# Counting subsets of both node halves with one pair of matmuls in a one-core graph network kernel

## The chip, the cores and the metric

The kernel runs on one core of a Trainium2 chip. The metric is the device time of one execution in microseconds (us). Three runs of the kernel before took 6450.48, 6465.61 and 6453.73 us, so its median is 6453.73 us. The engines are named as the profile names them: PE is the matrix engine (PEld its weight loads), DVE the vector engine, ACT the scalar engine, POOL the general engine that here also issues one DMA queue, and SP the engine that issues most other DMAs. PSUM is the memory that PE writes; it has eight banks of 512 fp32 columns on 128 partitions.

## The reference

There are 16 graphs of 1024 nodes with 128 features and a dense 0/1 adjacency matrix each. Four layers follow one another, each as `x = layernorm(x + layer(x, adj))`. Layer 0 is masked attention, layer 2 a sum over neighbours with a two-layer network, layer 3 a three-step convolution on a thinned adjacency matrix. The change touches layer 1 only:

```python
p = jnp.einsum('bnd,do->bno', x, W1 - W2)
q = jnp.einsum('bnd,do->bno', x, W2)
pre = p[:, :, None, :] + q[:, None, :, :] + b
h = jax.nn.relu(pre) * adj[..., None]
return jnp.max(h, axis=2)
```

For each node and feature this is the maximum of `q` over the node's neighbours, added to `p`, with a floor of zero. A maximum over a masked set of 1024 rows is not a matrix product, and the kernel finds it in another way.

## The kernel before, in words

The neighbours are taken in groups of six. A group has 64 subsets. For each group the kernel keeps a table with the maximum of `q` over each of the 64 subsets (128 features by 64 subsets), and for each node it needs the one entry that stands for the node's own neighbours in that group. Two groups (12 neighbours) make a slot: one on partitions 0 to 63, the other on partitions 64 to 127. A graph has `NP` = 86 slots, and all graphs together 16 x 86 = 1376.

One slot has these steps; the line numbers are those of the profile.

- `count` (L792): a matmul of a constant table of plus and minus ones, `lit`, with 120 rows of the transposed adjacency matrix, `AT`, gives for each subset and node the count of agreeing neighbours in `pm` (L799). ACT turns it into a one-hot row, `relu(count + 1 - size)`, written to `hot` (L800); the constant is the bias operand `one_less`. This is done twice in a slot, for nodes 0 to 511 and for nodes 512 to 1023, which are called its two halves, h = 0 and h = 1.
- `table` (L802), once in two slots: two PE transposes bring two slots' tables from `sub` into the PSUM tile `pt` (L811), and ACT copies it, rounded, to `high` (L814).
- `low_part` (L817): a matmul with minus the identity subtracts `high` from `pt` where it stands (L819), and ACT copies the rest to `low` (L821). `pt` so stays in its bank from `table` until `low_part` of the next slot's first half.
- `look_up` (L824), once for each half: four matmuls (L830) multiply `hot` by `high` and by `low`. The two groups lie on partitions 0 to 63 and 64 to 127 and use the two row halves of PE's array, into two banks of `pg`. DVE then keeps the running maximum in `best` (L890), 128x1024 in one instruction.

PSUM is laid out by tags: `wide` has two buffers of two banks for `pg`, `shared` two banks for the other layers, and `subset` two banks that `pm` and `pt` take in turn.

The counting runs two slots ahead of the look-up. The order of all work of PE, ACT, DVE and POOL in this stage is written out by the function `slot`: in each half come the look-up, then pieces of the other layers' work for PE ("streams": attention of the next graph, layer 2 of the last graph, and the thinning of the adjacency matrix, "dilation"), then their pieces for ACT and DVE, then `low_part`, `count` and `table`, then the maximum. Each engine runs its list strictly in that order, and an engine that waits for another holds up all that stands behind.

Chunks of `AT`, 120 rows for 10 slots, are loaded by POOL's DMA queue (L751), which converts fp32 to fp8. There are nine chunks for a graph (the last has 64 rows, and POOL clears its tile first, L750), four buffers, and a load is issued two chunks ahead of its use. The same engine, POOL, computes the row-by-row thinning (L658 to L668) and issues the loads of `An` and `E`.

After the 1376 slots come layer 3's passes over all graphs, which the change does not touch.

Of the kernel before, what the change touches and what calls it, by code (L numbers as in the profile page):

```python
# [29 lines left out]
F32 = mybir.dt.float32  # L30
F32R = mybir.dt.float32r
BF = mybir.dt.bfloat16
F8 = mybir.dt.float8e4
F16 = mybir.dt.float16
AF = mybir.ActivationFunctionType
# [4 lines left out]
B, N, D, H2 = 16, 1024, 128, 256  # L40
P = 128
T = N // P
GS = 6
PS = 2 * GS
PC = 10
CH = PC * PS
NP = -(-N // PS)
TG = 12
R, G = 32, 4
# [11 lines left out]
def subset_tables():  # L61

    half = P // 2
    s = np.arange(half)
    lit = np.zeros((CH, PC, P), np.float32)
    for j in range(CH):
        a, k = divmod(j % PS, GS)
        lit[j, j // PS, a * half:(a + 1) * half] = np.where((s >> k) & 1, 1.0, -1.0)
    size = sum((s >> k) & 1 for k in range(GS))
    return lit, np.tile(1.0 - size, 2).astype(np.float32).reshape(P, 1)  # L70


@with_exitstack
def tile_graph_layers(ctx: ExitStack, tc, a, out):
    nc = tc.nc
    x, adj, adjT = a["x"], a["adj"], a["adjT"]
    halves = (slice(0, 512), slice(512, 1024))

    consts = ctx.enter_context(tc.tile_pool(name="consts", bufs=1))
    dram = ctx.enter_context(tc.tile_pool(name="dram", bufs=1, space=DRAM))  # L80
    small = ctx.enter_context(tc.tile_pool(name="small", bufs=3))
    psum = None
# [9 lines left out]
    psum = setup.enter_context(tc.tile_pool(name="psum0", bufs=2, space=PSUM))  # L92
# [9 lines left out]
    nc.vector.memset(ones_b, 1.0)  # L102
    mhalf = consts.tile([P, T], F32, name="mhalf")
    nc.vector.memset(mhalf, -0.5)
    lit = consts.tile([CH, PC, P], F8, name="lit")
    nc.gpsimd.dma_start(out=lit, in_=a["lit"])
    less = consts.tile([P, P], F32R, name="less")
    nc.vector.tensor_scalar_mul(less, ident, -1.0)
    one_less = consts.tile([P, 1], F32, name="one_less")
    nc.sync.dma_start(out=one_less, in_=a["one_less"])  # L110

    def weight(name, shape=(P, P), how=None, pool=consts):
        t = pool.tile(list(shape), F32, name="w_" + name)
# [49 lines left out]
    pm = bank("pm")  # L163
# [5 lines left out]
    for b in range(B):  # L169
        q, g = divmod(b, G)  # L170
        nc.gpsimd.dma_start(out=half_rows[g * R:(g + 1) * R, :, q],
                            in_=a["nodemask"][b].rearrange("(k r) -> r k", r=R))
# [65 lines left out]
    def layers_012():  # L238
# [3 lines left out]
        psum = psums.enter_context(tc.tile_pool(name="psumA", bufs=1, space=PSUM))  # L242
        apool = es.enter_context(tc.tile_pool(name="apool", bufs=1))
# [500 lines left out]
        def load_columns(at):  # L744
            b, c = divmod(at, T + 1)
            if b < B:
                rows = min(CH, N - c * CH)
                t = AT[at] = apool.tile([CH, N], F8, name="AT", bufs=4)
                if rows < CH:
                    nc.gpsimd.memset(t, 0.0)  # L750
                nc.gpsimd.dma_start(out=t[:rows], in_=adjT[b, c * CH:c * CH + rows])  # L751

        An, AT, subs, qs, ps, values, exps, bests, hots, tables = ({} for _ in range(10))
        now, taken, given, held = 0, 0, {}, {}
        pending = {}
# [33 lines left out]
                        given[held[stream]] = now + 0.5  # L789
                    pending[stream] = [next(stream, None), now]  # L790

        def count(s, h):  # L792

            b, g = divmod(s, NP)
            c, r = divmod(g, PC)
            if h == 0:
                hots[s] = w2.tile([P, N], F32R, name="hot", bufs=3)
            pm = psum.tile([P, 512], F32, tag="subset", name="pm", bufs=2)
            nc.tensor.matmul(pm, lit[:, r, :], AT[b * (T + 1) + c][:, halves[h]], start=True, stop=True)  # L799
            nc.scalar.activation(hots[s][:, halves[h]], pm, AF.Relu, bias=one_less)  # L800

        def table(s):  # L802

            b, g = divmod(s, NP)
            g0 = g - g % TG
            assert ("sub", b, g0) in happened, (s, [(x.__name__, pending[x]) for x in streams], room)
            pt = psum.tile([P, 512], F32, tag="subset", name="pt", bufs=2)[:, :2 * P]
            if g + 2 - g0 == min(TG, NP - g0):
                happened["used", b, g0] = now
            for k in range(2):  # L810
                nc.tensor.matmul(pt[:, k * P:(k + 1) * P], subs[b, g0][:, g - g0 + k, :], ident, is_transpose=True,  # L811
                                 start=(k == 0), stop=(k == 1))
            high = w2.tile([P, 2 * P], F32R, name="high", bufs=2)
            nc.scalar.copy(high, pt)  # L814
            tables[s] = pt, high

        def low_part(s):  # L817
            pt, high = tables[s]
            nc.tensor.matmul(pt, less, high, start=False, stop=True, skip_group_check=True)  # L819
            low = w2.tile([P, 2 * P], F32R, name="low", bufs=2)  # L820
            nc.scalar.copy(low, pt)  # L821
            tables[s] = high, low

        def look_up(s, h, pg):  # L824

# [23 lines left out]
        def slot(s, last):  # L849

            nonlocal now
            now = s
            b, g = divmod(s, NP)
            if s >= 0 and g == 0:
                finish(b)
                if b + 1 < B:
                    start(tables_of(b + 1), True)
                    load_x(b + 1)
                    start(attend(b + 1))
                    start(scores(b + 1))  # L860
                if b:
                    start(rest(b - 1))
            if s >= 0 and g % PC == 0:
                load_columns(b * (T + 1) + g // PC + 2)
            for h in range(2):
                now = s + 0.5 * h
                for e in ROOM:
                    room[e] = min(room[e] + ROOM[e] / 2, ROOM[e])
                if s >= 0:
                    pg = psum.tile([P, 2, 512], F32, tag="wide", name="pg", bufs=2)  # L870
                    look_up(s, h, pg)
                early = s >= 0 and due < now
                if early:
                    dilate_on()
                advance(("PE",))
                advance(("A", "V", "Pool"))
                if s >= 0 and not early:
                    dilate_on()
                if h == 0 and s % 2 and s + 1 < last:
                    low_part(s + 1)  # L880
                if s + 2 < last:
                    count(s + 2, h)
                    if h and s % 2 == 0:
                        table(s + 2)
                if s >= 0:
                    own = bests[b][:, :, halves[h]]
                    if g == 0:
                        nc.vector.tensor_copy(own, pg)
                    else:
                        nc.vector.tensor_max(own, own, pg)  # L890
            if s >= 0:
                hots.pop(s)
# [1 line left out]
        dilate = dilation()  # L894
        due, wants_bank = 0.0, False
        load_x(0)
        for at in range(2):
            load_columns(at)
        front, back = scores(0), attend(0)
        for t in range(T):  # L900
            while ("e", 0, t) not in happened:
# [6 lines left out]
        first = tables_of(0)  # L908
# [2 lines left out]
        start(first, True)  # L911
        with tc.manual_schedule(engines={mybir.EngineType.PE, mybir.EngineType.Activation, mybir.EngineType.DVE,
                                         mybir.EngineType.Pool}):
            for s in range(-2, B * NP):
                slot(s, B * NP)
            finish(B)
        assert not streams, streams
# [316 lines left out]
```

## Time and profile before

| What | Value |
| --- | --- |
| profiled execution, its own time | 6458.95 us |
| its span, first to last instruction | 6457.2 us |
| median of the three runs | 6453.73 us |
| the slots' stage, first transposition of a table to the last one-hot | 129.9 to 5163.4 us, 5033.5 us |
| one slot, mean | 5033.5 / 1376 = 3.66 us |
| granted PE clock, whole span and slots' stage | 0.934 and 0.94 |
| first counting matmul | 36.8 us |

The profile is one execution. Busy time is given as the union of an engine's instructions, so a group with two matmuls at a time counts once. A PE matmul's recorded duration includes the time until its results are written, which overlaps the next matmul; so the distance from one start to the next says what a matmul costs PE, and a PE that is 92% busy in this sense still has room. "Idle before, releaser" says what ended an engine's idle time.

### The profile page before, as it was taken

Reading aid. Unit: us, or ns where it says so; the run is one execution under the profiler, and the core shown is the slowest. Engines: PE = TensorE matmul, PEld = TensorE weight load, DVE = VectorE, ACT = ScalarE, POOL = GpSimd, SP = SyncE. Lnnn points to the kernel's source line nnn. Section 1 sums busy time; section 2 is a strip of 40 time slices with the busy share of each in tenths; the row PEclk is TensorE's granted clock in tenths of the full one; section 3 lists DMA queues with packets and bytes.
Section 4 is the critical chain, followed back from the end, with each engine's and each line's share of the span. In section 5 each row is a group of like instructions: output and inputs, shape, how many; then the busy total and the mean of one; then the engine's idle time right before and its main releaser. Section 6 shows DMA issues by size and latency. Waiting matters only on the chain. (4 is left out here: it accounts for less than half of the span.)

```text
span 6457.2 us, 90620 instructions
## 1 busy us (share of the span) xinstructions
PE 5729.3 (89%) x29184; PEld 2962.2 (46%) x29354; DVE 4978.8 (77%) x7877; ACT 3946.3 (61%) x7142; POOL 3502.1 (54%) x11319
## 2 busy tenths in 40 slices
PE   6989999989899999999989998989998867877998
PEld 3444444444444444444444444444443335555654
DVE  3888888888888888888888888888888834444445
ACT  4667666666667666766666666666665623333755
POOL 2665766666666666766666666666666511110113
PEclk8989899999899999999999999998998988888999
DMA  5121212121212121212121212121211065654545
GB/s 38 13 30 21 35 21 36 21 34 21 34 21 37 20 35 20 34 20 32 24 34 20 34 20 34 20 35 20 35 21 18 20 101 106 126 103 111 206 167 186
DMA packets 478402, 317.32 MB, mean 49 GB/s; under 512 B 301162, under 2 KB 429668, under 8 KB 473828
## 3 DMA queue, kind: packets, MB, share of 16 engines
q0 software_dynamic: 105648, 84.20, 15.0%
q1 hardware_dynamic: 367600, 226.13, 11.9%
q8 instruction: 230, 3.77, 0.2%
q10 hardware_dynamic: 4676, 1.19, 0.1%
q14 instruction: 248, 2.03, 0.1%
HBM read 412.71 MB, written 117.18 MB: 82 GB/s over the span
## 5 line engine op out<-in xcount | busy, mean ns | idle before, releaser
L890 DVE TENSOR_TENSOR best<-best,pg 128x1024 f32<-128x1024 f32 x2720 | 3258.7, 1215 | 556.8 <-PE pg L830 546.8
L800 ACT ACTIVATE hot<-pm,one_less 128x512 fp32r<-128x512 f32 x2752 | 1882.7, 689 | 736.9 <-PE pm L799 727.5
L830 PE MATMUL pg<-hot,high 64*128 64x512 f32 x5504 | 1436.1, 519 | 239.2 <-DVE best L890 231.4
L830 PE MATMUL pg<-hot,low 64*128 64x512 f32 x5504 | 1139.8, 411 | 0.0
L799 PE MATMUL pm<-AT,lit 120*128 120x512 fp8e4 x2752 | 1110.3, 404 | 20.9 <-ACT hot L800 8.5
L830 PEld LDWEIGHTS pg<-hot,high 64*128 64x128 f32 x5504 | 533.6, 191 | 1018.9 <-DVE best L890 510.5
L830 PEld LDWEIGHTS pg<-hot,low 64*128 64x128 f32 x5504 | 553.0, 198 | 0.0
L658 POOL TENSOR_SCALAR sc<-low_counts,half_mask,rest 16x1 f32<-16x1 f32 x992 | 351.8, 355 | 323.7 <-DVE rest L644 218.8
L799 PEld LDWEIGHTS <-lit 120*128 120x128 fp8e4 x2752 | 272.6, 99 | 520.5 <-issue 460.2
L663 POOL TENSOR_SCALAR sc<-sc 16x1 f32<-16x1 f32 x992 | 397.3, 401 | 105.1
L821 ACT CAST low<-pt 128x256 fp32r<-128x256 f32 x688 | 256.1, 372 | 258.2 <-PE pt L819 255.0
L1039 POOL TENSOR_TENSOR length<-length,mhalf 128x8 f32<-128x8 f32 x48 | 78.9, 1644 | 570.8 <-DVE length L1038 570.8
L660 POOL TENSOR_SCALAR sc<-sc 16x1 f32<-16x1 f32 x992 | 315.0, 318 | 107.7
L819 PE MATMUL pt<-high,less 128*128 128x256 f32 x688 | 294.1, 427 | 85.0 <-ACT high L814 78.2
L703 POOL TENSOR_SCALAR shifts<-centre 128x4 f32<-128x4 f32 x32 | 10.5, 327 | 656.9 <-DVE width L699 633.6
L665 POOL TENSOR_SCALAR hit<-V,sc 16x31 bf16<-16x31 bf16 (+30 forms) x992 | 361.1, 364 | 0.0
L666 POOL TENSOR_SCALAR last_rank<-V,sc 16x31 f32<-16x31 bf16 (+30 forms) x992 | 344.5, 347 | 0.0
L996 ACT CAST m<-near 128x1024 fp32r<-128x1024 fp8e4 x256 | 253.4, 1044 | 112.6 <-DVE near L965 59.6
L475 DVE TENSOR_TENSOR sub<-sub,q 128x24 f32<-128x24 f32 (+11 forms) x768 | 303.3, 396 | 24.0 <-ACT q L297 10.4
L811 PE MATMUL pt<-ident,sub 128*128 128x128 f32 x1376 | 286.1, 291 | 26.7 <-ACT hot L800 22.3
L385 PE MATMUL pav<-v,eT 128*128 128x128 f32 x2048 | 301.7, 293 | 2.1 <-ACT eT L378 2.1
L1009 PE MATMUL pagg<-m,high 128*128 128x512 f32 x768 | 277.3, 432 | 13.2 <-ACT high L1002 13.2
(268 smaller groups left out, 9754.6 us busy)
## 6 DMA issues: line engine op xcount, KB each, us to landing
removed<-gone SPq DMA_DIRECT2D x128, 256.0 KB
An<-in_adj_dram POOLq DMA_DIRECT2D x16, 1024.0 KB, 14.8
E<-in_adj_dram POOLq DMA_DIRECT2D x128, 128.0 KB, 5.8
gone_all<-removed POOLq DMA_DIRECT2D x64, 256.0 KB, 12.3
near<-in_adjT_dram POOLq DMA_DIRECT2D x16, 1024.0 KB, 17.9
kept<-near SPq DMA_DIRECT2D x16, 1024.0 KB
share<-share SPq DMA_DIRECT2D x32, 512.0 KB
hidden<-r SPq DMA_DIRECT2D x32, 512.0 KB
```

The costliest lines, as they stand in the source:

```text
L385: nc.tensor.matmul(pav, eT[:, c, :], values[b][:, c, :], start=(c == 0), stop=(c == T - 1))
L475: nc.vector.tensor_max(sub[:, :n_g, n:2 * n], sub[:, :n_g, 0:n], qg[:, 2 * g0:2 * g0 + n_g, k:k + 1].to_broadcast([P, n_g, n]))
L658: gp.tensor_scalar(half, mine, half_mask[:, m], rest[:, n:n + 1], op0=ALU.mult, op1=ALU.add)
L660: gp.tensor_scalar(sf, half, 5.5, sf, op0=ALU.is_gt, op1=ALU.mult)
L663: gp.tensor_scalar(to, at, sf, none, op0=ALU.subtract, op1=ALU.subtract)
L665: gp.tensor_scalar(hit[:, n, n + 1:], V[:, n, n + 1:], at, None, op0=ALU.is_equal)
L666: gp.tensor_scalar(last[:, n + 1:], V[:, n, n + 1:], to, None, op0=ALU.is_le)
L799: nc.tensor.matmul(pm, lit[:, r, :], AT[b * (T + 1) + c][:, halves[h]], start=True, stop=True)
L800: nc.scalar.activation(hots[s][:, halves[h]], pm, AF.Relu, bias=one_less)
L819: nc.tensor.matmul(pt, less, high, start=False, stop=True, skip_group_check=True)
L830: nc.tensor.matmul(pg[:, a], part[rows, at * P:(at + 1) * P], hots[s][rows, halves[h]], start=(k == 0), stop=(k == 1))
L890: nc.vector.tensor_max(own, own, pg)
```

## The change

`count` is done once for a slot. `lit` and `AT` become bf16 and are laid out anew: 60 neighbour rows of nodes 0 to 511 lie on partitions 0 to 59, and the same 60 neighbour rows of nodes 512 to 1023 on partitions 64 to 123. `lit` has the same table on both. Partitions 60 and 124 of `AT` hold ones, and those of `lit` the constant `1 - size`, so the bias operand goes. The two matmuls of 61 rows stand one after the other and are given the two row halves of PE's array; they write the two banks of one two-bank tile `pm`, and one ACT instruction of 128x1024 makes the whole `hot`.

That tile is the only buffer of the tag `subset`. The table can no longer stay in its bank between `high` and `low`, so the tables are transposed twice: once for `high` (`high_part`), and once more, one slot later, for `low` (`low_part`), followed at once by the subtraction. In a slot `count` stands at the end of the first half, and `high_part` (odd slots) or `low_part` (even slots) at the end of the second. `high_part` stands one slot earlier than `table` did, and the stage's loop begins one slot earlier.

The chunks of `AT` have two buffers in place of four, whose rows of ones are set once, and are loaded one chunk ahead in place of two. A chunk is two DMAs (four for a graph's last chunk), and the clearing of the last chunk's tile is gone. Two one-row DMAs of `one_less` into `lit` come at the start.

```diff
-    lit = consts.tile([CH, PC, P], F8, name="lit")
+    lit = consts.tile([P, PC // 2, P], BF, name="lit")
     nc.gpsimd.dma_start(out=lit, in_=a["lit"])
+    for part in range(2):
+        nc.gpsimd.dma_start(out=lit[64 * part + SUB:64 * part + SUB + 1],
+                            in_=a["one_less"].rearrange("(o r) m -> o r m", o=1))
...
-                t = AT[at] = apool.tile([CH, N], F8, name="AT", bufs=4)
-                if rows < CH:
-                    nc.gpsimd.memset(t, 0.0)
-                nc.gpsimd.dma_start(out=t[:rows], in_=adjT[b, c * CH:c * CH + rows])
+                t = AT[at] = columns_in[at % len(columns_in)]
+                for part, s in enumerate(halves):
+                    whole = rows // SUB
+                    first = c * CH + whole * SUB
+                    nc.gpsimd.dma_start(out=t[64 * part:64 * part + SUB, :whole],
+                                        in_=adjT[b, c * CH:first, s].rearrange("(j r) m -> r j m", r=SUB))
...
+        columns_in = [apool.tile([P, 2, 512], BF, name=f"AT{i}") for i in range(2)]
+        for t in columns_in:
+            nc.vector.memset(t, 1.0)
...
-            pm = psum.tile([P, 512], F32, tag="subset", name="pm", bufs=2)
-            nc.tensor.matmul(pm, lit[:, r, :], AT[b * (T + 1) + c][:, halves[h]], start=True, stop=True)
-            nc.scalar.activation(hots[s][:, halves[h]], pm, AF.Relu, bias=one_less)
+            pm = both_banks("pm")
+            for part in range(2):
+                rows = slice(64 * part, 64 * part + SUB + 1)
+                nc.tensor.matmul(pm[:, part], lit[rows, r, :], AT[b * (T + 1) + c][rows, j, :], start=True, stop=True)
+            nc.scalar.activation(hots[s], pm.rearrange("p h n -> p (h n)"), AF.Relu)
...
+        def both_banks(name):
+            return psum.tile([P, 2, 512], F32, tag="subset", name=name, bufs=1)
...
+        def high_part(s):
+            pt = turned(s)
+            tables[s] = w2.tile([P, 2 * P], F32R, name="high", bufs=2)
+            nc.scalar.copy(tables[s], pt)
...
         def low_part(s):
-            pt, high = tables[s]
-            nc.tensor.matmul(pt, less, high, start=False, stop=True, skip_group_check=True)
+            pt = turned(s)
+            nc.tensor.matmul(pt, less, tables[s], start=False, stop=True, skip_group_check=True)
...
-                load_columns(b * (T + 1) + g // PC + 2)
+                load_columns(b * (T + 1) + g // PC + 1)
...
-                if h == 0 and s % 2 and s + 1 < last:
-                    low_part(s + 1)
-                if s + 2 < last:
-                    count(s + 2, h)
-                    if h and s % 2 == 0:
-                        table(s + 2)
+                if h == 0:
+                    if 0 <= s + 2 < last:
+                        count(s + 2)
+                elif s % 2:
+                    if s + 3 < last:
+                        high_part(s + 3)
+                elif s + 2 < last:
+                    low_part(s + 2)
```

`turned` is the part of the old `table` that takes the PSUM tile and does the two transposes (L811).

## The prediction

> **What bounds the kernel now.** I read the page first, then the slots' stage by itself, then the waits, and last PE's own list in order of time.
>
> ```profile
> L890 DVE TENSOR_TENSOR best<-best,pg 128x1024 f32<-128x1024 f32 x2720 | 3258.7, 1215 | 556.8 <-PE pg L830 546.8
> L800 ACT ACTIVATE hot<-pm,one_less 128x512 fp32r<-128x512 f32 x2752 | 1882.7, 689 | 736.9 <-PE pm L799 727.5
> ...
> L819 PE MATMUL pt<-high,less 128*128 128x256 f32 x688 | 294.1, 427 | 85.0 <-ACT high L814 78.2
> ...
> L811 PE MATMUL pt<-ident,sub 128*128 128x128 f32 x1376 | 286.1, 291 | 26.7 <-ACT hot L800 22.3
> ```
>
> ```profile
> core 0: us, PE busy (x) PEld busy (x) DVE busy (x) ACT busy (x) POOL busy (x), PEclk, DMA share, GB/s
> 130.00:5163.00 5033.00, 4597.58 (x24012) 2257.17 (x24178) 4362.48 (x6692) 3333.43 (x6298) 3266.30 (x10896) 0.94 0.19 26
> ```
>
> In the slots' stage (the second view) PE is recorded busy 91% of the time, DVE 87%, ACT 66%, POOL 65%. A slot takes 3.66 us; DVE has 4362.5 / 1376 = 3.17 us of work in it. In this view neither PE nor DVE alone is full: they wait for each other in turn, since `pg` has only two buffers.
>
> ```profile
> POOL shifts L703 <- DVE width L699: 633.6, 31, 33.2
> ...
> DVE best L890 <- PE pg L830: 546.8, 951, 7.7
> PEld pg L830 <- DVE best L890: 510.5, 920, 5.8
> ...
> PE pg L830 <- DVE best L890: 231.4, 238, 5.5
> ```
>
> The waits give total, times and the longest, in us. DVE waited for PE 951 times and a weight load of PE for DVE 920 times. So a microsecond saved or added on PE reaches the end only where PE is the later of the two, roughly every second time. ACT is off the path save where PE waits for a bank (78.2 and 22.3 us).
>
> ```profile
> 2505.49 0.38 PE L799 MATMUL pm<-AT,lit 120*128 120x512 fp8e4 x1
> 2505.80 0.50 PE L830 MATMUL pg<-hot,high 64*128 64x512 f32 x2
> 2506.14 0.40 PE L830 MATMUL pg<-hot,low 64*128 64x512 f32 x2
> 2506.47 0.39 PE L799 MATMUL pm<-AT,lit 120*128 120x512 fp8e4 x1
> 2506.79 0.50 PE L830 MATMUL pg<-hot,high 64*128 64x512 f32 x2
> 2507.12 0.40 PE L830 MATMUL pg<-hot,low 64*128 64x512 f32 x2
> 2507.45 0.82 PE L427 MATMUL pa<-An,parts 128*128 128x512 fp8e4 x3
> 2508.11 0.38 PE L799 MATMUL pm<-AT,lit 120*128 120x512 fp8e4 x1
> 2508.33 0.38 PE L811 MATMUL pt<-ident,sub 128*128 128x128 f32 x2
> 2508.64 0.50 PE L830 MATMUL pg<-hot,high 64*128 64x512 f32 x2
> ```
>
> The lines give start and duration in us. From start to start: a count before a look-up costs PE 0.32 us (2506.47 to 2506.79), before another full-array matmul 0.22; a look-up pair 0.33; two transposes 0.31. A half with nothing between count and count but a look-up lasts 0.98 us (2505.49 to 2506.47).
>
> **The change, part by part.** "Gross" is what PE gains or loses; "passed" what reaches the end.
>
> 1. PE's work. In two slots four counts become two pairs. A pair costs what one count did, if it runs as the look-up's pairs do (x2 in 0.33 us). Two counts go, 2 x 0.32, and one pair of transposes comes, 0.31: 0.33 us less for two slots, 688 x 0.33 = 227 us gross. Setting each of DVE's waits before L890 against what PE would save ahead of it, the smaller of the two sums to 88 us (0.083 us in each half) or 168 us (0.165). I take -130.
>
> 2. Row halves next to row halves. The count before a look-up costs 0.10 us more than before a full-array matmul, and the step from look-up to count 0.33, 0.11 more than 0.22. In some 20% of slots no stream work lies between look-up and count in the first half, and there both extras go: 1376 x 0.20 x 0.21 = 58 us gross, between 0 and 58; taken -30. The Trainium skill (TensorEngine Tiling (Array Packing), Tiling Modes, Key Properties) says that a change of tiling mode drains the array; by that rule the whole 58 us goes. The rows show the 0.10 and 0.11 us, but not what a bf16 pair costs beside the fp32 one.
>
> 3. The old wait of the subtraction for `high` (78.2 us) goes, since `high` is copied a slot earlier. By the same half, -45 (between 0 and -78).
>
> 4. The new wait. With one buffer, `turned` at the end of the second half cannot start until ACT has read all of `pm`, which PE wrote half a slot earlier. The new ACT instruction is not in the trace. ACT's relu from PSUM without bias takes 597 ns for 512 columns (L323), and 1114 ns against 687 ns is the step from 512 to 1024 columns with a bias (L1025, L299): 597 + 427 = 1.02 us. From the pair's start it is 0.39 (matmul) + 0.04 (ACT starts 37 ns after PE's end) + 1.02 + 0.055 (PE starts after ACT) = 1.50 us before PE may transpose. PE gets there after 0.98 us where only a look-up lies between. Lined up slot by slot in the trace, the time from a slot's first count to its second had quartiles 0.99, 1.59 and 1.98 us. With each first one-hot's end put 0.33 us later (1.02 for 0.69), PE would come too early in 59% of slots, and wait 424 us gross. Behind the waiting transposes stand the next slot's look-up on PE, and DVE's maximum behind that. Where DVE was still busy at that maximum the wait is covered: taking its slack off leaves 225 us passed at once. Below: ACT has 0.36 us a slot less to do (2 x 0.689 - 1.02), so a one-hot that stood behind other ACT work starts sooner; 0.2 us sooner leaves 282 gross, 140 passed. Above: all 424. I take +225, as lateness not passed at once is in part passed later.
>
> 5. A second wait: the next count must wait until ACT has copied `high` or `low` out of the same tile, and that copy (0.37 us) stands behind the second half's stream work on ACT. Lined up likewise: 57 us gross in 8% of slots, 27 passed; taken +27.
>
> 6. ACT's saving, 0.36 x 1376 = 495 us busy, is worth nothing by itself: ACT already waits 727.5 us for counts.
>
> 7. Loads. 144 issues at 0.66 us become 16 x (8 x 2 + 4) = 320: 116 us more on POOL, less 16 clearings of 0.94. That is 3.3 us in each of 31 blocks of thinning, under the 20 us that POOL waits for `width` in each (633.6 / 31): 0. A chunk is asked for 8 slots (29 us) ahead, a graph's first chunk 4 slots (14.6 us), and needs two issues and a landing, 2 x 0.66 + 3.8 = 5.1 us. POOL issued the four-slot loads between 18 us before and 4 us after their slot began: covered. (Near the end it was up to 22 us late, against 29 us.) If that cover went, each load late by 1 us would stop PE's count and cost up to 143 us in all. POOL ahead of its slot now waits for PE's last count in the buffer that it refills, and the thinning rows behind it lose only lead. SP loses one issue.
>
> 8. The start. Two one-row issues and a wait for `lit` to land stand ahead of POOL's other loads; ACT waited 5.6 us for the first `An`. Between 0 and 8 us, taken +3. DVE's two memsets and the extra first slot fall into this idle time.
>
> Sum: -130 - 30 - 45 + 225 + 27 + 3 = +50 us on the profiled 6458.95, 6509; the median of the runs lies 5.2 us lower, so 6505 us, 0.8% slower.
>
> Against this change the Trainium skill speaks twice (Perfetto Trace Analysis): Optimizing Tensor Performance, Matmuls, wants independent matmul groups to rotate through PSUM banks so that evacuation overlaps the next group, and Optimizing Scalar/DVE Operations wants larger instructions where the engine is saturated and smaller ones where an unsaturated engine makes others wait. ACT at 66% is the latter; by the rule the bubble stays whole, 424 + 57 in place of 225 + 27, and the time would be 6733. The trace has DVE cover half of it.
>
> **Rivals.**
>
> - Faster: the wait mostly does not come. For it: ACT's list gets shorter, and it waited 727.5 us for counts. Against it: 0.98 against 1.50 us in the shortest halves, which no shorter ACT queue mends. It decides where the wait passes less than the 205 - 30 = 175 us of items 1 to 3 less items 5 and 8. At 140 passed, nothing for item 5 and all of 168, 58 and 78: -161, 6293; halfway to the forecast about 6400.
> - Much slower: PE becomes later than DVE nearly everywhere, and all of items 4 and 5 passes: 424 + 57 - 130 - 30 - 45 + 3 = +279, 6733. For it: one tile makes PE and ACT alternate in every half. Against it: DVE's 3.17 us of work a slot.
> - The pairs do not overlap, so a pair costs 0.22 more: 1376 x 0.22 = 303 gross, half passed, about 6655. Against it: the look-up's pairs on the same row halves.
> - Loads late: 143 loads by 1 to 3 us, 6600 to 6900. Against it: item 7.
>
> **How the numbers follow.** This kernel's measurement can tell 0.3%, 19 us, from no change. Chances: forecast 0.48 (0.39 of it slower, 0.08 same, 0.01 faster), faster rival 0.27 (0.26 faster, 0.01 same), much slower 0.18, pairs 0.03, loads 0.04. Together slower 0.64, same 0.09, faster 0.27. The range, 6370 to 6690, leaves out a tenth on each side: the faster rival's far half and the upper part of the slower ones. The forecast's own range is 6440 to 6610.
>
> **What would show it.** In the changed profile: the relu of 128x1024 near 1.02 us; counts x2 with 0.33 us to the look-up; a wait "PE pt <- ACT hot" of 300 to 450 us in place of 22.3, mostly behind halves without streams; no wait of the subtraction for `high`; DVE's wait for `pg` above 546.8 us; ACT near 55% in the stage; no wait of a count for a DMA. The prediction is wrong if the wait for `hot` stays under 150 us, if a look-up after a count starts later than 0.4 us, or if a count waits for a load.

## The result, and the profile after

The changed kernel took 6508.34 us (median of 4 runs, 6502.60 to 6518.97) against 6454.54 us (4 runs, 6450.48 to 6465.61) for the kernel before: a ratio of 1.0083, 95% interval 1.0064 to 1.0101, so 54 us or 0.8% slower. The prediction was 6505. The profiled execution was the longest of the four, 6518.97 us, with a span of 6515.7 us. The times below are those of fast executions; one of the four of e10_apart_noturn took 9151.69 us and is left out of its time.

The page of the changed kernel, its first line and the costliest groups of instructions (busy time, mean ns of one, then the idle time before them and its releaser):

```profile
span 6515.7 us, 92909 instructions
...
L912 DVE TENSOR_TENSOR best<-best,pg 128x1024 f32<-128x1024 f32 x2720 | 3264.2, 1215 | 620.3 <-PE pg L850 604.8
L815 ACT ACTIVATE hot<-pm 128x1024 fp32r<-128x1024 f32 x1376 | 1407.1, 1023 | 815.4 <-PE pm L814 811.9
...
L824 PE MATMUL pt<-ident,sub 128*128 128x128 f32 x2752 | 611.8, 306 | 465.9 <-ACT hot L815 460.7
...
L814 PE MATMUL pm<-AT,lit 61*128 61x512 bf16 x2752 | 570.6, 410 | 30.2 <-ACT high L831 22.6
```

The single ACT instruction for a slot's one-hots takes 1023 ns, and PE's transpositions now wait 460.7 us for it, where the same row of the kernel before had 22.3. No row of the subtraction (L835) waits for `high` any more, and no count waits for a load.

Busy times in the slots' stage of the changed kernel:

```profile
core 0: us, PE busy (x) PEld busy (x) DVE busy (x) ACT busy (x) POOL busy (x), PEclk, DMA share, GB/s
130.00:5220.00 5090.00, 4327.59 (x25537) 2309.62 (x25537) 4365.11 (x6679) 3001.71 (x4920) 3385.42 (x11055) 0.93 0.19 29
```

PE's busy share fell from 91% to 85% and ACT's from 66% to 59%, and yet the stage is longer. DVE's work is what it was, 4365 against 4362 us.

The waits of the changed kernel (total, times, longest, in us):

```profile
PEld pt L824 <- ACT hot L815: 898.9, 1041, 2.8
ACT hot L815 <- PE pm L814: 811.9, 808, 4.2
DVE best L912 <- PE pg L850: 604.8, 1008, 9.7
...
POOL shifts L705 <- DVE width L701: 532.9, 32, 27.5
PE pt L824 <- ACT hot L815: 460.7, 713, 2.3
...
PEld pg L850 <- DVE best L912: 309.5, 377, 5.8
...
PE pg L850 <- DVE best L912: 209.1, 210, 5.6
...
POOL AT L754 <- PE pm L814: 126.9, 29, 21.4
```

DVE waits longer for PE than before (604.8 against 546.8), and PE's weight loads wait less for DVE (309.5 against 510.5): PE is now the later of the two more often, by a wait that was 22.3 us before.

PE's list in order of time (start, duration, in us):

```profile
2500.93 0.39 PE L814 MATMUL pm<-AT,lit 61*128 61x512 bf16 x2
2500.97 0.59 PE L850 MATMUL pg<-hot,high 64*128 64x512 f32 x2
2501.39 0.39 PE L850 MATMUL pg<-hot,low 64*128 64x512 f32 x2
2502.52 0.44 PE L824 MATMUL pt<-ident,sub 128*128 128x128 f32 x2 [0.74 <-ACT hot L815]
2502.89 0.50 PE L850 MATMUL pg<-hot,high 64*128 64x512 f32 x2
```

Two things are to be seen. A pair of counts costs PE very little in front of a look-up: from its start to the `low` pair 0.46 us, where one count had 0.65 (2505.49 to 2506.14 in the kernel before). And the transposition starts 1.59 us after the counts, though PE could have been there after 0.46 + 0.33 = 0.79.

**Where the time went, on PE's own row.** The steps from the start of one PE matmul to the start of the next add up to the whole time. I read these steps from the records between 400 and 4800 us. A step's own length was taken as the shortest usual one between the same two neighbours (the 5th percentile over all kernels of this study; for the step to a `low` pair behind a count the median, 0.42, since it scatters); the rest of a step is lateness of the matmul that ends it. In us per slot, with some of the experiments told below:

```
                              before  after  e1_apart  e2_first  e8_later  e9_both  e7_full
time of a slot                 3.706  3.730     3.568     3.756     3.670    3.623    3.702
PE's own work                  3.073  2.741     2.715     2.820     2.653    2.610    3.181
late: transpositions           0.049  0.446     0.173     0.200     0.181    0.098    0.088
late: subtraction              0.083  0         0         0         0        0        0
late: look-up (high pair)      0.241  0.267     0.369     0.305     0.329    0.372    0.204
late: counts                   0.061  0.047     0.091     0.160     0.272    0.273    0.052
the rest                       0.199  0.229     0.220     0.271     0.235    0.270    0.177
```

The change took 0.332 us a slot of work off PE (457 us over 1376 slots) and 0.083 of the old wait (114 us), and it added 0.397 us of lateness of the transpositions (546 us). These nearly cancel; the look-up, the counts and the rest make the small difference. The rows of lateness hardly depend on how the neighbours are grouped, but the line between PE's own work and the rest does: grouped otherwise, up to 0.1 us a slot moves from one to the other, and the work saved comes to 0.29 to 0.34. The stage lost its time gradually, and none in its last third: set against the kernel before, slot 86 ended 12 us later, slot 600 32 us, slot 946 58 us, slot 1375 59 us, and layer 3 behind it took as long as before.

### The profile page after: what moved, and what is told of

The parts are those of the page before. It is cut to its first block, busy times and chain, and to the rows that moved or that the text cites. A ratio compares the mean times of both kernels' runs of the same rounds, so it can differ in the third digit from the quotient of the medians.

```text
span 6515.7 us, 92909 instructions
## 1 busy us (share of the span) xinstructions
PE 5461.6 (84%) x30730; PEld 3014.8 (46%) x30730; DVE 4987.6 (77%) x7879; ACT 3616.6 (56%) x5766; POOL 3623.7 (56%) x11481
## 5 line engine op out<-in xcount | busy, mean ns | idle before, releaser
L912 DVE TENSOR_TENSOR best<-best,pg 128x1024 f32<-128x1024 f32 x2720 | 3264.2, 1215 | 620.3 <-PE pg L850 604.8
L815 ACT ACTIVATE hot<-pm 128x1024 fp32r<-128x1024 f32 x1376 | 1407.1, 1023 | 815.4 <-PE pm L814 811.9
L850 PE MATMUL pg<-hot,high 64*128 64x512 f32 x5504 | 1566.9, 565 | 217.0 <-DVE best L912 209.1
L850 PE MATMUL pg<-hot,low 64*128 64x512 f32 x5504 | 1153.8, 415 | 0.0
L824 PE MATMUL pt<-ident,sub 128*128 128x128 f32 x2752 | 611.8, 306 | 465.9 <-ACT hot L815 460.7
L850 PEld LDWEIGHTS pg<-hot,high 64*128 64x128 f32 x5504 | 558.8, 199 | 502.8 <-DVE best L912 309.5
L824 PEld LDWEIGHTS pt<-ident,sub 128*128 128x128 f32 x2752 | 312.7, 147 | 947.6 <-ACT hot L815 898.9
L814 PE MATMUL pm<-AT,lit 61*128 61x512 bf16 x2752 | 570.6, 410 | 30.2 <-ACT high L831 22.6
L831 ACT CAST high<-pt 128x256 fp32r<-128x256 f32 x688 | 255.5, 371 | 235.8 <-PE pt L824 227.8
L814 PEld LDWEIGHTS <-lit 61*128 61x128 bf16 x2752 | 148.9, 96 | 482.4 <-issue 451.5
```

The lines of the kernel that those rows point to most:

```text
L814: nc.tensor.matmul(pm[:, part], lit[rows, r, :], AT[b * (T + 1) + c][rows, j, :], start=True, stop=True)
L815: nc.scalar.activation(hots[s], pm.rearrange("p h n -> p (h n)"), AF.Relu)
L850: nc.tensor.matmul(pg[:, a], part[rows, at * P:(at + 1) * P], hots[s][rows, halves[h]], start=(k == 0), stop=(k == 1))
```

## Experiments

The theory: with one buffer of two banks, PE's transposition waits for ACT to read both banks, and this wait is what the change costs; most of it passes to the end. The rivals: the wait is harmless, and something else costs the time (the second transposition, the more numerous loads one chunk ahead, the granted clock), or the wait only takes back what the row halves give. All edits are to the changed kernel, and all ratios are to the kernel before.

**e1_apart: two buffers of one bank.** The same two banks, but each a buffer of its own; ACT reads them in two instructions, and the transposition needs only the first.

```diff
-            return psum.tile([P, 2, 512], F32, tag="subset", name=name, bufs=1)
+            return psum.tile([P, 512], F32, tag="subset", name=name, bufs=2)
...
-            pm = both_banks("pm")
+            pm = [one_bank("pm") for part in range(2)]
...
-            nc.scalar.activation(hots[s], pm.rearrange("p h n -> p (h n)"), AF.Relu)
+            for part in range(2):
+                nc.scalar.activation(hots[s][:, halves[part]], pm[part], AF.Relu)
...
-            pt = both_banks("pt")[:, 0, :2 * P]
+            pt = one_bank("pt")[:, :2 * P]
```

> The two halves of pm become two one-bank tiles, each with its own relu of 128x512; the table's transposes then need only the first of the two reads to be done: 0.39 + 0.04 + 0.60 + 0.055 = 1.09 us after the counts start, in place of 1.50. Theory (PE stands before the transposes until all of pm is read, and about half of that reaches the end): the wait PE pt <- ACT hot falls from 460.7 us to 100 to 200, and the time to 6340 to 6420 us, although ACT gets 0.17 us a slot more to do. Rival (the wait is covered by DVE, and what costs is the added loads or the second transposition): 6490 to 6530 us.

Measured: 6294.61 us (6284.33 to 6298.03), ratio 0.9749 (0.9727 to 0.977). The page's groups of this kernel:

```profile
L913 DVE TENSOR_TENSOR best<-best,pg 128x1024 f32<-128x1024 f32 x2720 | 3246.4, 1214 | 403.6 <-PE pg L851 388.2
L816 ACT ACTIVATE hot<-pm 128x512 fp32r<-128x512 f32 x2752 | 1496.4, 597 | 713.0 <-PE pm L814 709.0
L851 PE MATMUL pg<-hot,high 64*128 64x512 f32 x5504 | 1529.1, 549 | 311.9 <-DVE best L913 294.0
...
L825 PE MATMUL pt<-ident,sub 128*128 128x128 f32 x2752 | 592.2, 298 | 137.3 <-ACT hot L816 129.1
```

The wait fell by 332 us, to 129.1, and the time by (1.0083 - 0.9749) x 6454 = 216 us, 65% of it, which is more than the half that was expected. ACT is busy for longer than in the changed kernel (1496.4 against 1407.1 us for the one-hots), and the kernel is 3.3% faster than it (0.9749 / 1.0083 = 0.967) and 2.5% faster than the kernel before. In the table the lateness of the transpositions fell by 0.273, and that of look-ups and counts rose by 0.102 and 0.044: where PE comes sooner, DVE is the later one (PE's look-ups wait 294.0 us for `best`, against 209.1).

**e4_twice: the two reads without the two buffers.** One tile as in the change, read by ACT in two instructions.

```diff
-            nc.scalar.activation(hots[s], pm.rearrange("p h n -> p (h n)"), AF.Relu)
+            for part in range(2):
+                nc.scalar.activation(hots[s][:, halves[part]], pm[:, part], AF.Relu)
```

> The one tile pm stays, but is read by two relus of 128x512 in place of one of 128x1024: 1.15 to 1.19 us in place of 1.02, with the same result. Theory: the wait PE pt <- ACT hot rises from 460.7 us by about 0.15 x 0.6 x 1376 = 120 us, and the time by half of it, to 6540 to 6600 us. Rival (the wait is covered, loads or transposes cost): 6490 to 6530 us.

Measured: 6547.11 us (6541.25 to 6552.44), ratio 1.0142 (1.0121 to 1.0163). The wait of this kernel:

```profile
PE pt L825 <- ACT hot L816: 517.8, 739, 2.5
```

It rose by 57 us, and the time by 0.0059 x 6454 = 38 us. So smaller instructions alone cost time; it is the bank given back sooner that pays.

The Trainium skill (Perfetto Trace Analysis, Optimizing Scalar/DVE Operations) advises smaller instructions where an unsaturated engine makes another wait. Here that held only together with its other advice (Optimizing Tensor Performance, Matmuls) to rotate matmul groups through banks: 0.9749 with both, 1.0142 with the split alone.

**e3_short: the read half as long, the buffer unchanged.** ACT reads one bank only, and both halves' look-ups use its one-hots.

```diff
-            nc.scalar.activation(hots[s], pm.rearrange("p h n -> p (h n)"), AF.Relu)
+            nc.scalar.activation(hots[s][:, :512], pm[:, 0], AF.Relu)
...
-                    nc.tensor.matmul(pg[:, a], part[rows, at * P:(at + 1) * P], hots[s][rows, halves[h]],
+                    nc.tensor.matmul(pg[:, a], part[rows, at * P:(at + 1) * P], hots[s][rows, halves[0]],
```

> The relu reads one bank of pm only and writes half of hot; both halves' look-ups read that half, so the one-hot rows of nodes 512 to 1023 are left out. All PE work, transposes and loads stay. The read takes 0.60 us in place of 1.02. Theory: the wait PE pt <- ACT hot falls from 460.7 us to 100 to 200 and the time to 6320 to 6420 us. Rival (added loads or second transposition): 6490 to 6530 us.

Measured: 6291.88 us (6288.80 to 6297.03), ratio 0.9748 (0.9728 to 0.9768), again below the range expected. The wait of this kernel:

```profile
PE pt L824 <- ACT hot L815: 155.2, 411, 1.9
```

A shorter read and an earlier release of the bank are worth the same here, which fits that it is the time to that release that counts. Three runs that move mainly this wait (e1 down 332 us, e3 down 305, e4 up 57) moved the time by 65%, 71% and 67% of it. Each moves something else too: e1 gives ACT 89 us more to do, and e3 takes away half of its reading. The intervals leave the share of e4 anywhere between some 35 and 100%.

**e2_first: the count sooner, right behind the first half's look-up.** More time then passes from count to transposition.

```diff
+                if h == 0 and 0 <= s + 2 < last:
+                    count(s + 2)
...
-                if h == 0:
-                    if 0 <= s + 2 < last:
-                        count(s + 2)
...
```

> The counts of a slot stand right behind the first half's look-up, ahead of that half's stream work, so the stream work of both halves lies between the counts and the transposes; nothing else changes. Theory: the wait PE pt <- ACT hot falls from 460.7 us to under 150, the count's wait for the copies of high and low rises from 27 us to 50 to 200, and the time is 6350 to 6440 us. Rival (added loads or second transposition): 6490 to 6530 us, since both stay.

Measured: 6540.16 us (6525.72 to 6542.10), ratio 1.0125 (1.0098 to 1.0153). A miss: it was slower than the changed kernel. The waits of this kernel:

```profile
DVE best L911 <- PE pg L850: 587.5, 906, 11.9
...
PE pt L824 <- ACT hot L815: 180.4, 308, 1.1
...
PE pm L814 <- ACT high L831: 60.8, 137, 12.7
...
PE pm L814 <- ACT low L837: 49.1, 75, 5.0
```

The wait for the one-hots fell by 280 us as it should, but the buffer's other user now waits: the counts come before ACT has copied `high` or `low` out (0.160 us a slot late in the table, against 0.047). PE's own work also rose, by 0.08 us a slot. Its list shows where:

```profile
2509.43 0.39 PE L814 MATMUL pm<-AT,lit 61*128 61x512 bf16 x2
2509.76 1.12 PE L339 MATMUL psc<-kT,qT 128*128 128x512 f32 x2
```

Ahead of a full-array matmul the pair costs 0.33 us, ahead of a look-up 0.13 (0.04 to the `high` pair, and 0.42 in place of 0.33 from there to the `low` pair). The lower lateness of the transpositions, 0.246 us a slot, and 0.026 more so went to the counts (0.113), PE's own work (0.079), the look-ups (0.038) and the rest (0.042).

**e8_later: the transposition later, the count where it was.** The transpositions and the subtraction move half a slot back, behind the next first half's look-up.

```diff
+                if h == 0 and s >= -2:
+                    if s % 2 == 0:
+                        if s + 2 < last:
+                            high_part(s + 2)
+                    elif s + 1 < last:
+                        low_part(s + 1)
...
-                elif s % 2:
-                    if s + 3 < last:
-                        high_part(s + 3)
-                elif s + 2 < last:
-                    low_part(s + 2)
```

> The changed kernel with its single two-bank tile, but the table's transposes and the subtraction stand half a slot later, behind the next first half's look-up and ahead of its stream work, so a whole further look-up lies between the counts and the transposes; ACT's copies stand ahead of that half's stream work too. Theory: the wait PE pt <- ACT hot falls under 100 us, the counts' wait for the copies rises from 27 to 100 to 250 us, and the time is 6240 to 6380 us. Rival (order within the slot matters little, as with e2_first, and only the banks do): 6480 to 6550 us.

Measured: 6420.16 us (6417.57 to 6422.55), ratio 0.9935 (0.992 to 0.9949), between the two expectations. The waits of this kernel:

```profile
PE pm L814 <- ACT high L831: 164.5, 322, 11.7
...
PE pm L814 <- ACT low L837: 156.9, 334, 4.0
...
PE pt L824 <- ACT hot L815: 96.6, 301, 1.4
```

Moving the transposition away from one wait moves it into another: 364 us less of the old one, and some 300 more of the counts for the copies, above the 250 expected. With the buffer shared, one of its two users stands close behind the other; this order is the cheaper, and even beats the kernel before.

**e9_both: the two buffers and the later transposition.** The edits of e1_apart and e8_later together:

```diff
...
+            return psum.tile([P, 512], F32, tag="subset", name=name, bufs=2)
...
+                            high_part(s + 2)
+                    elif s + 1 < last:
+                        low_part(s + 1)
...
```

> The edits of e1_apart and e8_later together: two one-bank tiles, and the table's transposes half a slot later. Theory (e1_apart has brought PE's waits down so far that DVE, 89% busy in its stage, is mostly the later one): 6270 to 6320 us, about e1_apart's 6295, with the wait PE pt <- ACT hot under 40 us. Rival (what is left of the waits still passes at two thirds): 6200 to 6260 us.

Measured: 6348.43 us (6346.40 to 6351.27), ratio 0.9832 (0.9816 to 0.9847): a miss, 0.8% slower than e1_apart alone. The table shows the exchange: 0.075 less lateness of the transpositions and 0.055 less of own work and the rest together, but 0.182 more lateness of the counts. The waits view puts only some 42 us of that on ACT's copies (31.0 and 11.4 us). The order of time shows more:

```profile
2510.95 0.36 PE L836 MATMUL pt<-high,less 128*128 128x256 f32 x1
2511.24 0.90 PE L814 MATMUL pm<-AT,lit 61*128 61x512 bf16 x2
2511.35 0.37 ACT L838 CAST low<-pt 128x256 fp32r<-128x256 f32 x1 [1.63 <-PE pt L836]
2511.77 0.60 PE L851 MATMUL pg<-hot,high 64*128 64x512 f32 x2
```

Here two counts take 0.90 us, since the second starts at 2511.77, 0.05 us after ACT has copied `low` out of `pt`. Three tiles (`pt` and the two of `pm`) take two buffers in turn, so the second count gets the buffer that the transposition just ahead of it has filled. Most of this wait lies under the first count's record of 0.39 us. By the records between 400 and 4800 us, 310 of the 331 us that the counts were late fell on second counts that started within 0.09 us of the end of such a copy; in the changed kernel no second count was late.

**e7_full: the old counts in the new order.** Two full-array counts of 120 rows a slot, with the bias operand, and loads of whole chunks two ahead, as in the kernel before; order and buffers as in e1_apart.

```diff
-    lit = consts.tile([P, PC // 2, P], BF, name="lit")
+    lit = consts.tile([CH, PC, P], F8, name="lit")
...
-                t = AT[at] = columns_in[at % len(columns_in)]
+                t = AT[at] = apool.tile([CH, N], F8, name="AT", bufs=4)
...
+            pm = [psum.tile([P, 512], F32, tag="subset", name="pm", bufs=2) for h in range(2)]
+            for h in range(2):
+                nc.tensor.matmul(pm[h], lit[:, r, :], AT[b * (T + 1) + c][:, halves[h]], start=True, stop=True)
+            for h in range(2):
+                nc.scalar.activation(hots[s][:, halves[h]], pm[h], AF.Relu, bias=one_less)
...
-                load_columns(b * (T + 1) + g // PC + 1)
+                load_columns(b * (T + 1) + g // PC + 2)
```

> As e1_apart in order and buffers, but the counts are those of the kernel before: 120 rows on the whole array, fp8, one after the other at the end of the first half, relu with the bias operand, loads two chunks ahead. Theory (the row halves save PE about 0.3 us a slot: 0.215 + 0.216 + 0.316 + 0.332 from the stream work to the low matmuls in the trace of before against 0.311 + 0.036 + 0.422 in the changed one; two thirds pass): 6295 + 1376 x 0.31 x 0.67 = 6580, 6520 to 6640 us. Rival (the row halves are worth little, and the gain of e1_apart came from its buffers and its order alone): 6290 to 6360 us.

Measured: 6460.90 us (6453.96 to 6464.26, 10 runs), ratio 0.9995 (0.9986 to 1.0005), between theory and rival. So the second transposition and the new order, taken together and at a clock of 0.944 to 0.948, neither gain nor lose beside the kernel before, and all of the 2.5% of e1_apart comes from what e7_full lacks: the row halves, with the form of bias and loads that belongs to them. That is (0.9995 - 0.9749) x 6454 = 159 us out of 0.466 us a slot, 641 us, of PE's own work: only about a quarter of it reached the end.

**e5_noturn: without the second transposition.** `low` is computed from the subtraction alone, so its low-order part is left out.

```diff
-            pt = turned(s)
-            nc.tensor.matmul(pt, less, tables[s], start=False, stop=True, skip_group_check=True)
+            pt = both_banks("pt")[:, 0, :2 * P]
+            nc.tensor.matmul(pt, less, tables[s], start=True, stop=True)
```

> low_part takes its PSUM tile and multiplies minus the identity by high into it, without transposing the table a second time; so low is minus high, and the table's low-order part is left out. The subtraction now waits for hot where the transposes did. Theory (the second transposition costs PE 0.19 us each time, 2505.91 to 2506.10 in the changed kernel's trace, and two thirds of PE's time passes, as the first runs gave): 688 x 0.19 x 0.67 = 88 us less, 6400 to 6450 us. Rival (it is hidden, DVE covers it): 6490 to 6530 us.

Measured: 6503.24 us (6494.57 to 6510.50), ratio 1.0066 (1.0048 to 1.0083). The theory missed, the rival held: the time hardly changed. The waits of this kernel show one reason:

```profile
PE pt L824 <- ACT hot L815: 217.6, 360, 2.3
...
PE pt L835 <- ACT hot L815: 207.6, 339, 2.4
```

The subtraction takes the transposition's place behind the same buffer, and the wait is 217.6 + 207.6 = 425 us against 460.7. The other thing to be seen is the clock:

```profile
core 0: 6495.0 us, clock 0.901
```

It was 0.897 to 0.903 in all of this kernel's runs, and 0.924 to 0.929 in those of the changed kernel.

**e11_data: the same numbers, with the work.** Both transpositions stay, but the subtraction overwrites their result, so `low` has the values of e5_noturn.

```diff
-            nc.tensor.matmul(pt, less, tables[s], start=False, stop=True, skip_group_check=True)
+            nc.tensor.matmul(pt, less, tables[s], start=True, stop=True)
```

> The changed kernel with every instruction as it was, but the subtraction overwrites the transposed table in place of adding to it, so low is minus high as in e5_noturn; the low-order part is left out, and no work. If the lower clock of e5_noturn came from the missing transposes: 6500 to 6520 us with a clock near 0.927. If it came from the other numbers that then run through PE: a clock near 0.90 and 6560 to 6620 us, and the second transposition's cost is then the difference to e5_noturn's 6503.

Measured: 6497.36 us (6492.10 to 6518.53), ratio 1.0068 (1.0045 to 1.0091), clock 0.925 to 0.930: the first expectation, its time missed by 3 us. So it was the missing transpositions that lowered the clock in e5_noturn, not the numbers, and the two kernels take the same time: in the changed kernel the second transposition costs nothing that can be measured, taken with the lower clock that came when it was left out.

**e10_apart_noturn: e5_noturn's edit on top of e1_apart.** Again the low-order part of `low` is left out.

```diff
-            pt = turned(s)
-            nc.tensor.matmul(pt, less, tables[s], start=False, stop=True, skip_group_check=True)
+            pt = one_bank("pt")[:, :2 * P]
+            nc.tensor.matmul(pt, less, tables[s], start=True, stop=True)
```

> e1_apart without the second transposition, as e5_noturn did it: low is minus high, and the table's low-order part is left out. In e5_noturn the time fell by 0.2% only and PE's granted clock from 0.927 to 0.90. Theory (the second transposition costs PE 131 us, but without it PE is granted a lower clock): 6260 to 6300 us with a clock near 0.90. Rival (in the changed kernel the wait for hot had covered it, and here it shows): 6190 to 6240 us with a clock near 0.93.

Measured: 6263.35 us (three executions, 6259.96 to 6266.26), ratio 0.9697 (0.9673 to 0.9721), clock 0.919 to 0.922: the theory's time, with a clock between the two that were named. With most of the wait out of the way leaving out the second transposition gains 0.5%, 0.0052 x 6454 = 34 us, again with the lower clock; the intervals of the two kernels lie just apart (up to 0.9721, and from 0.9727).

**e6_noload: nearly no loads.** Only the first two chunks are loaded; all other counts read them again, so 316 of 320 issues are left out and counts belong to wrong rows.

```diff
+                if at > 1:
+                    AT[at] = columns_in[at % len(columns_in)]
+                    return
```

> Only the first two chunks of the transposed adjacency matrix are loaded; all later counts use them again, so the counts belong to the wrong rows and 316 of the 320 load issues, their transfers and POOL's waits for a free buffer (127 us in the changed kernel) are left out. Theory (loads are hidden): 6490 to 6520 us. Rival (the loads, issued later and in twice the pieces, cost the 54 us): 6440 to 6470 us.

Measured: 6490.67 us (6483.22 to 6493.50), ratio 1.0042 (1.0027 to 1.0057), at the lower edge of the theory's range. Without the loads the kernel took 0.0041 x 6454 = 27 us less; the intervals of this kernel and the changed one lie just apart (up to 1.0057, and from 1.0064). The waits of this kernel:

```profile
POOL shifts L705 <- DVE width L701: 723.0, 32, 44.5
DVE best L915 <- PE pg L853: 579.7, 982, 6.0
...
PE pt L827 <- ACT hot L818: 463.4, 713, 2.5
```

The wait for the one-hots is untouched. POOL, without its issues and without its 126.9 us of waiting for old chunks to be read, comes to its wait for `width` earlier and stands there 190 us longer. Why DVE then waits 25 us less for PE was not shown. The granted clock was higher, 0.931 to 0.932 in place of 0.924 to 0.929, so how much of the 27 us is the loads' own is open.

**The granted clock.** No run changes it alone, but the executions on record bound this rival. The kernel before was executed 27 times beside these experiments. It took 6442.16 us at a clock of 0.936 and 6472.61 us at 0.931, and a line through all 27 gives 4.9 us for each 0.001 of clock; one through the four of the changed kernel gives 3.1 us. On average the changed kernel's clock was 0.007 lower than that of the kernel before. If the clock acts between the two kernels as it does among the executions of one, some 20 to 35 us of the 54 go with it; that is an estimate from these figures. The table agrees: the lateness of the look-ups and the rest in steps that began at full clock is 0.311 us a slot before and 0.305 after, and in steps that began at half clock 0.133 and 0.179. The large moves are not the clock's: e4_twice had a higher clock than the changed kernel (0.928 to 0.932) and was slower, and by the same estimate the clock of e1_apart, 0.930 to 0.933, is worth 15 to 20 us of its 216. Whether the lower clock is a cause of the 54 us or only follows from PE's waiting, no run shows.

## Why the prediction was right, point by point

The number was right to 4 us (the sum as written gives 6504), and the mechanism named for it, ACT's read of a two-bank buffer, is the one that the experiments e1, e3 and e4 move. But several terms were too small, and they cancelled; that it came so close is luck.

1. Items 1 and 2, PE's work. Predicted 227 + 58 = 285 us gross; measured 457. The step that failed is "a pair costs what one count did": ahead of a look-up it costs 0.13 us, not 0.32; by how much the whole saving exceeded the 285 depends on the grouping of the steps (some 400 to 470 us). The Trainium skill (TensorEngine Tiling (Array Packing), Tiling Modes, Key Properties) says that changing the tiling mode drains the array. The runs fit this: from a pair on row halves to the next on row halves 0.04 us, from there to a full-array matmul 0.33 (e2_first), and from a full-array `pa` matmul to a count 0.31 where it had been 0.22. Behind a look-up it is the other way round: the counts start 0.23 us after the `low` pair (2509.20 to 2509.43 in e2_first), where a full-array count started after 0.33, so the extra of item 2 did go. The prediction weighed the rule for 58 us and left out its larger use, in the price of the pair itself.

2. Item 4, the new wait. Predicted 424 us gross; the waits view has 460.7 in place of 22.3, and by PE's steps it is 546 more. The buffer came free about as worked out (1.59 us after the counts' start in the lines shown, against 1.50). What was wrong is PE's arrival: 0.98 us predicted, 0.79 measured, because the pair is cheap. So in the slots where no stream work lies between (504 of 1180 in the stretch read, with 71% of the lateness) the pair's unforeseen saving went straight into the wait. This is why these two wrong terms nearly cancelled: they have one cause.

3. Item 3, the subtraction's wait, went as predicted; it was 78.2 us in the waits view and 114 by PE's steps.

4. Item 5, the counts' wait for the copies. Predicted 57 us gross. It did not come: 22.6 + 4.4 us in the changed kernel, and the counts are late by no more than before (0.047 against 0.061 us a slot). It is real all the same, and appears as soon as the count or the transposition moves (110 us in e2_first, 321 in e8_later).

5. "Roughly every second time". For this wait the share that passed was 65 to 71%, not 53% (225 of 424). For PE's own work it was 25% (e7_full against e1_apart). One share for all terms was wrong, and so is the sum built on it: with the measured sizes, half of -457 + 546 - 114 - 19 would give -22 us, not the +54 measured, and with 25% for work and 68% for waits it would be -114 + 280 = +166. The shares are no constants, and the sum of +54 is not derived from its terms by any of these runs; that stays open. What is shown is that taking away most of the one wait turns +0.8% into -2.5%. The prediction also had no term for the granted clock, which fell by 0.007.

6. Item 6, ACT's saving of 495 us, taken as nothing. Right, and more than that: e1_apart gives a part of it back (89 us of busy time) and is faster. ACT's busy time in the stage fell by 332 us only, to 59% where near 55% was named.

7. Item 7, the loads, taken as covered. No count waited for a load, as predicted, but e6_noload took 27 us less without them, half of the loss; by which way, and how much of it through the clock, is not shown. The cover named (POOL's 20 us of waiting in each block) holds for POOL's own row only.

8. Item 8, the start: +3 predicted. The first transposition came at 125.3 us against 129.9, and the first slot ended within 0.2 us of the one before: nothing.

Of the rivals, "faster" failed by its own condition: the wait passed more than 175 us (taking away 332 us of it moved the end by 216). "Much slower" assumed that nothing is covered; about a third was. "Pairs don't overlap" was refuted by 0.46 against 0.65 us. "Loads late" did not happen in the changed kernel; in e1_apart, which is faster, counts waited for loads 5 times, 10.1 us in all. Of the signs named, the look-up's start after a count (0.33 us predicted, 0.04 measured) was the one that should have been read first, since it reaches into both large terms.

## What to carry to other kernels

When a change saves work on an engine and puts a buffer's release behind that work, the saving arrives at the release sooner and waits there; cost the two together, by when the buffer comes free, not one by one. Before one large read of a shared buffer is accepted for its lower busy time, try the same banks as separate buffers with a read each: here 89 us more of busy time on ACT bought 3.3%. The version to keep is e1_apart, 6294.61 us.

## What the runs showed of the hardware

- Two 61-row bf16 matmuls on the two row halves, followed by a look-up on the same row halves, cost PE 0.13 us; the same pair followed by full-array work 0.33.
- Splitting a 128x1024 ACT read of PSUM into two of 128x512 costs 2 x 597 - 1023 = 171 ns each time by mean durations, but only 89 us more busy time in 1376 slots (65 ns each), so successive ACT instructions overlap in the records.
- The granted clock differed between kernels of nearly the same time: 0.924 to 0.929 with both transpositions, 0.897 to 0.903 without the second, 0.944 to 0.948 with full-array counts (e7_full, time of the kernel before). The values of `low` made no difference (0.925 to 0.930 with those of e5_noturn). It does not go by PE's busy share alone: between 400 and 4600 us that was 84% in e4_twice (clock 0.928 to 0.932) and 85% in e5_noturn.
- In the trace the clock is granted in full or at half, with nothing between. Between 400 and 4800 us of the changed kernel it was at half in 71 stretches of 3.4 us or a multiple, though PE sat idle for longer than 3.4 us only 4 times there.
